# Turning tiles through DRAM instead of on TensorE in a four-layer graph kernel, with a fifth pair under way and an order by fitted keys

## Chip, cores, metric

One core of a Trainium2 chip. The metric is device time in us, the median of several executions. Every timed kernel ran on the same chip as runs of the kernel before. The runs are spread over several chips; the kernel before has medians of 3864.35 to 3866.42 us on them, so times from different chips compare to some 2 us. "Step" below always means the distance between successive elements of an operand within a partition, counted in fp32 elements of 4 bytes.

## The reference, cut

64 graphs of 256 nodes with 256 features pass four layers, each `x = x + layer(relu(layernorm(x)), adj)`, all in fp32:

```python
# layer 0: masked 8-head attention        q, k, v = h@Wq, h@Wk, h@Wv; softmax(where(adj>0, q k^T/sqrt(32), -1e9)) @ v @ Wo + bo
# layer 1: graph attention over columns   e = leaky(f1_i + f2_j); softmax over i; elu(att @ Wh)
# layer 2: gated graph network, 3 steps   m = A^T (h W_l);  h = GRU(m, h)
# layer 3: 4-head graph attention         probs = softmax(leaky(src_i + dst_j)); probs @ f
h = jnp.maximum(_layernorm(x, axis=-1), 0.0)
x = x + _L0_gnn_ref(h, adj, ...)     # and so on for layers 1, 2, 3
```

## The kernel before

Graphs are worked on in pairs, 512 tokens, as four chunks of 128 tokens; 32 pairs. Operations are added to a plan as tasks; a list scheduler in the host program fixes the order of all tasks on all engines, for four pairs under way at once (four token tiles `x`, thirty 128x1024 tiles `w4`). TensorE needs every normalised tile with features on the partitions, and layer 2's state with tokens on them. The kernel before gets both with TensorE's transposition:

```python
    def norm_relu_T(xt, p, tokens=False):
        ...                                       # statistics; xn = (x - mean) * rstd, tokens on partitions
        for k in range(2):
            ps = bank()
            def turn(k=k, ps=ps):                 # L554
                for t in range(T):
                    nc.tensor.transpose(ps()[:, t * P : (t + 1) * P], tok(xn())[:, t, k * P : (k + 1) * P], ident)
            add((PE, 4 * TURN, turn), reads=[xn], writes=[ps], claims=[hT])
            ...                                   # eviction with relu into hT[:, k, :], 512 tokens in a row
    def chunk(hT, k, t):                          # stationary operand: one chunk of 128 tokens
        return tok(hT(), N2)[:, k, t * P : (t + 1) * P]
    # layer 0, L662: mm(ps(), w[:, k, o*P:(o+1)*P], tok(hT(), N2)[:, k, :])        moving operand, 512 tokens
    # layer 2, L910: mm(ps(), w[:, k, c0:c0+P], at_o(src, k))                       moving operand, 512 tokens
    # layer 2, L891: mm(..., tok(h())[:, t, o*P:(o+1)*P], tok(am(), N)[:, t, :])    h as stationary operand
```

The attention probabilities of layers 0 and 3 were already turned in another way, by 32x32 blocks on VectorE and a round trip through DRAM that puts the blocks in their places:

```python
    def turn(e, eT, n):
        blocks = lambda: e().rearrange(f"p (r {n}) -> p r c i", c=2, i=32)
        add((V, dve(T * N), lambda: nc.vector.transpose(blocks(), blocks())), writes=[e])
        d = buf("turn")
        add((SP, 0.6, lambda: nc.sync.dma_start(d(), e())), reads=[e], writes=[d], latency=4.6)
        for b in range(4):
            add((SP, 0.55, lambda b=b: nc.sync.dma_start(
                    eT()[32 * b : 32 * b + 32, :].rearrange("p (a w) -> p a w", a=4),
                    d()[:, b * N : (b + 1) * N].rearrange("(a j) w -> j a w", a=4))),
                reads=[d], writes=[(eT, b)], latency=3.8)
```

## Time and profile before

| | before |
|---|---|
| time | 3866.03 us (3865.26 to 3868.96) |
| TensorE busy | 3785.4 us, 98% |
| VectorE, ScalarE busy | 77%, 57% |
| DMA queue's share of 16 engines; bytes | 45.9%; 554 MB |

In the views PE stands for TensorE's matmuls, PEld for its weight loads (they overlap matmuls), DVE for VectorE, ACT for ScalarE, POOL for GpSimd, SPq for SyncE's queue of transfers. L910 is line 910 of that run's kernel. A stretch view gives the stretch and its length, the busy us and count of PE, PEld, DVE, ACT and POOL, the granted clock, the DMA engines' share and GB/s.

Two rows of the groups by form (busy us, mean ns) are added for comparison with those after the change:

```profile
L910 PE MATMUL ps<-w,whhT 128*128 128x512 f32 x1536 | 725.2, 599 | 7.8 <-ACT w L336 7.5 <-DVE w L337 0.3
L788 PEld LDWEIGHTS ps<-w1a,w 128*128 128x128 f32 x512 | 97.2, 190 | 21.1 <-issue 7.2 <-ACT w L713 0.2 <-ACT w L563 0.2
```

TensorE's instructions in order of time (columns: start, length with the pipeline's drain, engine, line, operation, count). These are the query, key and value products:

```profile
2020.83 3.60 PE L662 MATMUL ps<-w,wq_sb 128*128 128x512 f32 x8
2024.26 3.60 PE L662 MATMUL ps<-w,wk_sb 128*128 128x512 f32 x8
2027.69 3.62 PE L581 MATMUL ps<-wv_sb,w 128*128 128x256 f32 x16
```

The cost of a group is the distance of its start from the next start: 3.43 us for eight, 0.429 us each. From such distances, each form's usual distance times its count, I get **3719 us of TensorE work** in the kernel before; the other 147 us of its 3866 are waits, most of them at the start and the end. (3719 is my reckoning from the trace; the rest of the text calls it "work", and time less work "waits".)

### The profile page before, as it was taken

The page shows a single profiled execution, that of the slowest core. Times are in us where ns is not written, and L with a number is a line of the kernel's source. Part 1 is how long each engine was busy: PE and PEld are TensorE (multiplying, and loading weights), DVE is VectorE, ACT ScalarE, POOL GpSimd, SP SyncE. Part 2 cuts the span into 40 slices and gives each one's busy share as a digit, 9 for nine tenths or more (in the row PEclk, how much of TensorE's full clock was granted, in tenths as well). Part 3 has the DMA queues.
Part 4 walks back from the last instruction along what each step waited for, and adds up shares of the span by engine and source line. Part 5 has one row for each costly group of instructions (what it writes and reads, how often), then busy time and mean ns, then how long its engine had stood idle before and what let it go on. Part 6 is the DMA issues. An engine that isn't in the chain of part 4 may idle for free.

```text
span 3862.9 us, 55709 instructions
## 1 busy us (share of the span) xinstructions
PE 3785.4 (98%) x17072; PEld 2286.4 (59%) x17072; DVE 2965.7 (77%) x8153; ACT 2211.7 (57%) x6139; POOL 673.9 (17%) x632
## 2 busy tenths in 40 slices
PE   8999999999999999999999999999999999999995
PEld 5665665565566566555666665656565665556553
DVE  7976778778877877787787788777787787877754
ACT  5745556555565555566555665555665556664632
POOL 1111211122111212111221112121111120111110
PEclk9999999999999999999999999999999999999997
DMA  7623444335453445453355444445544455444523
GB/s 226 186 92 102 153 148 152 125 120 178 158 156 113 150 137 164 151 167 124 116 163 159 156 131 149 138 145 169 154 126 132 133 176 164 149 135 122 157 66 99
DMA packets 402202, 554.29 MB, mean 143 GB/s; under 512 B 40304, under 2 KB 340208, under 8 KB 401904
## 3 DMA queue, kind: packets, MB, share of 16 engines
q1 hardware_dynamic: 401904, 550.73, 45.9%
q8 instruction: 137, 2.24, 0.2%
q14 instruction: 161, 1.32, 0.1%
HBM read 332.15 MB, written 218.43 MB: 143 GB/s over the span
## 4 chain that ended last, share of the span: by engine, by line
PE 95%; ACT 2%; DVE 1%; DMA 1%; SPq 0%; issue 0%; POOL 0%; POOLq 0%; ACTq 0%; DVEq 0%
PE ps L910 34%; PE ps L990 17%; PE ps L891 9%; PE ps L581 5%; PE ps L662 5%; PE ps L682 3%; PE ps L732 3%; PE ps L1119 3%; PE ps L1076 3%; PE ps L788 3%; PE ps L554 3%; PE ps L846 3%; PE ps L976 2%; ACT w L638 1%; PE ps L1134 1%; PE ps L431 0%
## 5 line engine op out<-in xcount | busy, mean ns | idle before, releaser
L638 ACT ACTIVATE w<-w,mx 128x256 f32<-128x256 f32 x1536 | 758.2, 500 | 22.8 <-DVE mx L630 22.8
L910 PE MATMUL ps<-w,whhT 128*128 128x512 f32 x1536 | 725.2, 599 | 7.8 <-ACT w L336 7.5
L910 PE MATMUL ps<-w,giT 128*128 128x512 f32 x1536 | 718.8, 595 | 0.0
L336 ACT COPY w<-ps 128x512 f32<-128x512 f32 x516 | 293.0, 583 | 442.4 <-PE ps L891 155.0
L614 DVE STREAM_TRANSPOSE w<-w 128x1024 f32<-128x1024 f32 x384 | 473.3, 1239 | 56.4 <-ACT w L638 46.7
L910 PEld LDWEIGHTS ps<-w,giT 128*128 128x128 f32 x1536 | 287.1, 190 | 337.8 <-issue 323.6
L910 PEld LDWEIGHTS ps<-w,whhT 128*128 128x128 f32 x1536 | 278.3, 191 | 292.5 <-issue 259.3
L630 DVE CUSTOM_DVE_ANT_0 w<-ps,mask 128x256 f32<-128x256 f32 x1024 | 370.1, 418 | 78.9 <-PE ps L682 78.5
L947 POOL TENSOR_TENSOR w<-w,w 128x512 f32<-128x512 f32 x128 | 165.3, 1297 | 1169.1 <-ACT w L942 944.8
L990 PE MATMUL ps<-whhT,w 128*128 128x512 f32 (+1 forms) x1024 | 360.8, 489 | 0.0
L990 PE MATMUL ps<-giT,w 128*128 128x512 f32 (+1 forms) x1024 | 360.0, 488 | 0.0
L891 PE MATMUL ps<-w,w 128*128 128x256 f32 x1536 | 348.4, 379 | 0.0
L891 PEld LDWEIGHTS ps<-w,w 128*128 128x128 f32 x1536 | 290.8, 190 | 56.6 <-issue 15.8
L638 ACT ACTIVATION_READ_ACCUMULATOR w<-w,mx 128x1 f32 x1536 | 296.5, 193 | 0.0
L990 PEld LDWEIGHTS ps<-giT,w 128*128 128x128 f32 x1024 | 192.3, 190 | 150.7 <-issue 129.0
L1023 ACT ACTIVATE w<-w 128x512 f32<-128x512 f32 x128 | 80.4, 628 | 306.4 <-DVE w L1019 306.2
L990 PEld LDWEIGHTS ps<-whhT,w 128*128 128x128 f32 x1024 | 189.2, 190 | 108.1 <-issue 89.7
L713 ACT ACTIVATE w<-w,rz 128x256 f32<-128x256 f32 x506 | 220.1, 501 | 26.8 <-DVE rz L706 26.5
L1044 POOL TENSOR_TENSOR w<-w,w 128x512 f32<-128x512 f32 x64 | 83.5, 1305 | 787.4 <-ACT w L1043 717.5
L1097 ACT ACTIVATE w<-w,f 128x256 f32<-128x256 f32 x512 | 217.3, 501 | 5.7 <-DMA w<-row 5.7
L922 ACT ACTIVATE w<-ps,brz 128x512 f32<-128x512 f32 x128 | 87.5, 684 | 230.4 <-PE ps L910 230.4
L1019 DVE TENSOR_TENSOR w<-ps,brz_bc 128x512 f32<-128x512 f32 x128 | 87.5, 684 | 155.2 <-PE ps L990 141.6
(122 smaller groups left out, 6084.3 us busy)
## 6 DMA issues: line engine op xcount, KB each, us to landing
turn<-w SPq DMA_DIRECT2D x384, 512.0 KB
w<-turn SPq DMA_DIRECT2D x1536, 128.0 KB
w<-in_adj_dram SPq DMA_DIRECT2D x128, 512.0 KB
w<-row SPq DMA_DIRECT2D x64, 512.0 KB
x<-in_x_dram SPq DMA_DIRECT2D x64, 256.0 KB
out_dram<-x SPq DMA_DIRECT2D x64, 256.0 KB
w<-row SPq DMA_DIRECT2D x32, 256.0 KB
w<-in_L_gnn_weight_dram SPq DMA_DIRECT2D x3, 256.0 KB
```

Of the source, the lines that this page charges most:

```text
L336: (A, act(n), lambda: nc.scalar.copy(dst(), src())),
L581: mm(ps()[:, c * D : (c + 1) * D], of(src, k, 2 * g + c), rhs[:, k, :], start=k == 0, stop=k == 1)
L614: add((V, dve(T * N), lambda: nc.vector.transpose(blocks(), blocks())), writes=[e])
L630: nc.vector.tensor_tensor_reduce(row, cols(src), cols(mask), scale, 3.0e38, ALU.add, ALU.min, mn)
L638: nc.scalar.activation(row, row, AF.Exp, bias=mn()[:, r : r + 1], scale=-1.0, accum_out=zs()[:, z0(r) : z0(r) + 1])
L662: mm(ps(), w[:, k, o * P : (o + 1) * P], tok(hT(), N2)[:, k, :], start=k == 0, stop=k == 1)
L713: op(row, row, rz()[:, r : r + 1])
L891: mm(ps()[:, g * N : (g + 1) * N], tok(h())[:, t, o * P : (o + 1) * P], tok(am(), N)[:, t, :], start=c == 0, stop=c == 1,)
L910: mm(ps(), w[:, k, c0 : c0 + P], at_o(src, k), start=n == 0, stop=n == 2 * len(terms) - 1)
L947: either(lambda eng, o=o, u=u, hT=hT, hn=hn: eng.tensor_sub(at_o(u, o), at_o(hT, o), at_o(hn, o))),
L990: mm(out, chunk(src, k, t), w[:, k, c0 : c0 + n], start=m == 0, stop=m == 2 * len(terms) - 1)
L1097: (A, act(N, 1), lambda t=t, g=g, h=h, e=e, r=r: nc.scalar.activation(rows_of(e())[:, r].rearrange("p b (c j) -> p c b j", c=2), sd[g]().r ...
```

## The change

It means to take the turnings off TensorE, the bound. In all pairs but the first and the last, normalised tiles of all layers and layer 2's states after steps 1 and 2 take the way of the probabilities. A fifth pair goes under way to cover the longer latency, and the order comes from fitted constants instead of 36 trials. Core of the diff, cuts marked:

```diff
-        "x": (4, [P, T * D], FP, 0),
-        "w4": (30, [P, T * D], FP, 9),
+        "x": (5, [P, T * D], FP, 0),
+        "w4": (29, [P, T * D], FP, 9),
...
+    def by_dma(what, p):
+        return 0 < p < B // 2 - 1
...                                        # norm_relu_T
+        if mixed:
+            turn_chunks(xn, hT)
+            return (at, hT, xn) if tokens else (at, hT)
...
+    def turn_chunks(src, dst):
+        e = w4()
+        turn_blocks(
+            dict(reads=[src], writes=[e]),
+            lambda: src().rearrange("p (x b j) -> p b x j", b=4, j=32),
+            lambda: e().rearrange("p (b i x) -> p b x i", b=4, i=32), dst,
+        )
+        dst.mixed = True
...
     def chunk(hT, k, t):
+        if hT.mixed:
+            return hT().rearrange("p (n x) -> p x n", x=2 * T)[:, 2 * t + k]
         return tok(hT(), N2)[:, k, t * P : (t + 1) * P]
+    def wide(hT, k):
+        if hT.mixed:
+            return hT().rearrange("p (n t k) -> p k t n", t=T, k=2)[:, k]
+        return tok(tok(hT(), N2)[:, k, :], P)
...                                        # layer 0 query, key; layer 2 gates
-                        mm(ps(), w[:, k, o * P : (o + 1) * P], tok(hT(), N2)[:, k, :], ...)
+                        mm(ps(), w[:, k, o * P : (o + 1) * P], wide(hT, k), ...)
...                                        # layer 2, after steps 1 and 2
+            if by_dma((2, l), p):
+                turn_chunks(u, h)
+                continue
...
-    order = plan.best([(s, d, f) for s in range(5, 11) for d in (2, 3) for f in (...)])
+        for do in plan.order():            # one order, keys from PERIOD, REST, ON_PE, ON_SP, OTHERS
```

The relu moves into the scaling, on ScalarE. And the turned tile interleaves eight chunks: token `n` of chunk and half `x` lies at element `8 n + x`. So successive tokens are at **step 8**, 32 bytes, wherever TensorE reads the tile. The layout has a reason: a stationary operand may have only one free dimension (a first attempt of mine with runs of 32 tokens as stationary operand was refused at the build with those words; that build is not among the recorded runs), and step 8 makes a chunk's 128 tokens one dimension.

The cut leaves out three smaller changes: layer 0's masks and probabilities take the layout in halves that layer 3's had, its value product loses the step of 2 of its stationary operand, and layer 2's last step holds one large tile more (`df`).

## The prediction

> **What bounds the kernel now.** I read the page's busy shares first, then its slices, then the chain that ended last, then the busy time by stretch, and last the order of TensorE's instructions in time.
>
> ```profile
> PE 3785.4 (98%) x17072; PEld 2286.4 (59%) x17072; DVE 2965.7 (77%) x8153; ACT 2211.7 (57%) x6139; POOL 673.9 (17%) x632
> ...
> PE   8999999999999999999999999999999999999995
> ...
> PE 95%; ACT 2%; DVE 1%; DMA 1%; SPq 0%; issue 0%; POOL 0%; POOLq 0%; ACTq 0%; DVEq 0%
> PE ps L910 34%; PE ps L990 17%; PE ps L891 9%; PE ps L581 5%; PE ps L662 5%; PE ps L682 3%; PE ps L732 3%; PE ps L1119 3%; PE ps L1076 3%; PE ps L788 3%; PE ps L554 3%; PE ps L846 3%; PE ps L976 2%; ACT w L638 1%; PE ps L1134 1%; PE ps L431 0%
> ```
>
> TensorE is busy 98% of the span, but busy time of matmuls has modelled ends, so the third and fourth lines are the stronger evidence: the chain goes back along TensorE for 95% of the span and hops to another engine almost only at its ends. On it stand L554 (turning of the normalised tiles, 3%) and L976 (turning of layer 2's state back to tokens, 2%). These two lines are what the change takes away. The busy time by stretch tells where TensorE is not full (the first numbers after the comma are PE busy):
>
> ```profile
> 0.00:100.00 100.00, 82.58 (x440) 53.55 (x441) 75.26 (x269) 60.75 (x190) 13.88 (x20) 0.93 0.74 224
> 1000.00:2000.00 1000.00, 996.36 (x4535) 602.74 (x4534) 787.67 (x2155) 573.39 (x1600) 184.78 (x170) 1.00 0.47 147
> 3780.00:3863.00 83.00, 42.74 (x159) 25.22 (x157) 34.57 (x80) 21.95 (x61) 6.24 (x6) 0.72 0.27 83
> ```
>
> In the middle TensorE stands still for 4 us in 1000; at the start and the end it is idle for some 20 and 40 us. The two pairs that the change leaves on TensorE are the first and the last, so those ends keep their shape. The order in time shows what one turning costs the engine:
>
> ```profile
> 2017.36 1.04 PE L554 MATMUL ps<-ident,w 128*128 128x128 f32 x8
> 2018.24 1.04 PE L976 MATMUL ps<-ident,w 128*128 128x128 f32 x8
> 2019.11 1.88 PE L910 MATMUL ps<-w,whhT 128*128 128x512 f32 x4
> ```
>
> The 1.04 us is length with the pipeline's drain. What the next group has to wait is the difference of the starts: 0.88 and 0.87 us for eight, so **0.109 us of TensorE per 128x128 turning**. In the same way L910's 512 columns cost 1.72 us for four, 0.43 us each.
>
> **What the Trainium skill says.** "Trainium Kernel Development and Optimization" (introduction, on reading a trace) calls matmul busy time a bad measure because matmuls are pipelined. The trace agrees: the rows give 599 ns for a 512-column matmul whose starts are 430 ns apart. So I count by starts.
> "SBUF — State Buffer" (Door 1, the note on cachelines) states 16-byte lines, that two hits on a line are needed for full bandwidth, and that a new line at each access pays. This is the main danger: the change lays a turned tile out so that successive tokens of a chunk lie 8 fp32, 32 bytes, apart, and TensorE reads it so, as moving and as stationary operand. The trace before has only steps of 2 elements: L732 reads its moving tile so, and pays nothing against L1119, which reads runs (391 and 394 ns in the rows). The stationary tile of wv is read at step 2 too; its weight load takes 196 ns against 190 at step 1. No run yet shows step 8. "TensorE: Matmul & The Clock Gate" (Weight-path and gap formulas) gives N/2.4 ns plus 2.5 for a warm matmul, 216 ns for 512 columns; here 430 ns. fp32 streams at half that rate, so one fp32 access takes about the time of two accesses at the page's rate. My estimate from this is that a new line per access just fits.
> "GPSIMD Engine Reference" (Performance pitfalls for Q7 kernels) says a step above 8 bytes costs some 50% more per element. The subtractions at L947 and L1044 take 1.3 us now; no trace yet shows the wide step.
>
> **The change, part by part.**
> 1. *TensorE loses.* From the instruction lists of both programs: L554's turnings go from 1024 to 64, L976's from 512 to 32. That is 1440 x 0.109 = **157 us** of TensorE. All other matmul counts are the same. Per pair it is 48 x 0.109 = 5.2 us; the pattern of long L910 groups in the chain repeats at 2744.30, 2978.18, 3212.06, thus each 233.9 us for two pairs, 117 us a pair, and should become about 111.7.
> 2. *TensorE's reads change.* If step 8 is free, nothing. See rival 1.
> 3. *VectorE.* 180 more 32x32-block turnings (384 to 564) at 473.3/384 = 1.23 us: +222. 360 fewer scalings (384 to 24) at 177.9/384 = 0.46: -167. About 55 fewer evictions with maximum at 0.68: -37; 33 fewer plain evictions at 0.68: -22. 74 more divisions by the row sum at 0.31: +23; 90 more bias columns at 0.16: +15; the layer-0 mask in two halves: +6. Sum +40 us: 3006 us, 81% of 3706. Still slack.
> 4. *ScalarE.* 360 more scalings with relu at 66.6/128 = 0.52: +187; about 127 fewer relu evictions at 0.56: -71; 148 fewer copies at 0.57: -84; 74 fewer divisions at 0.43: -32. Sum near 0: 60%.
> 5. *DMA.* 180 more round trips through DRAM, 0.5 MB each way: 189 MB on 554, to 743 MB. Over 3706 us this is 200 GB/s against 143; with 45.9% of the engines' time at 143 GB/s I estimate 64%. SyncE issues 3267 transfers for 2367; at a median of 0.43 us that is 1.4 ms, 38%.
> 6. *Latency.* The last round trip of the kernel before, with nothing beside it, shows what one costs: the block turning ends at 3842.1 us, its matmul starts at 3849.2, so 7 us, against some 2 us for turning and eviction on TensorE. Six per pair lengthen a pair by about 30 to 40 us. This is paid in buffers, not in time, as long as other pairs have work: four pairs at 117 us gave a pair 468 us; five at 112 give 558, 90 more.
> 7. *Order.* Instead of 36 orders tried there is one with keys fitted beforehand. The middle has 4 us in 1000 to win; the ends, some 20 and 40 us, may move by 10 us either way.
>
> Sum on the path that sets the end: 3863 - 157 = 3706 us. For waits on round trips with 29 instead of 30 large buffers and at a heavier DMA I add about 10 us, and some 2 for runs without profile: **3715 us**, 4% faster.
>
> **The rivals.**
> *Rival 1: the step of 32 bytes slows TensorE.* Moving reads concerned: L662's 512 and half of L910's whhT (768), in 30 of 32 pairs: 1200 x 0.43 = 515 us at today's rate. At half the rate the program would take 3706 + 515 = 4220 us. For it: the skill's page. Against it: the half rate of fp32 above, and that the authors kept the old lengths for these matmuls in their plan. Weight loads at step 8 (wv, L788, L1076, two thirds of L891, some 2400) lie beside matmuls of 216 ns and would have to double before they show. I give rival 1 in a harmful size 10%.
> *Rival 2: the DMA becomes the wait.* Landings grow late under 64% load, SyncE's queue is in order, and a transfer that waits for its block turning holds those behind it. For it: the kernel before already shows
>
> ```profile
> SPq L616 <- DVE w L614: 1014.9, 207, 38.2
> ...
> SPq L619 <- DMA turn<-w: 127.8, 76, 4.4
> ```
>
> a queue that stands a quarter of the span at the head of a round trip. Against it: TensorE's own waits do not feel it; the only large wait for DMA on TensorE is 23.7 us in all, in the tail. If it bites once per pair for 2 us, 3770 us; that is a gain of 2.5%.
> *Rival 3: VectorE or the buffers become the bound.* Its turnings write at step 8, and if each took double, VectorE would have 3228 us, 87%: late answers to TensorE, perhaps 3750 us. If the 29 buffers can't carry five pairs, the middle gets holes and the gain is half: 3785 us.
>
> **Range and chances.** The arithmetic of the removed work is sure to a few us; what is open is how much comes back. Rivals 2 and 3 at moderate size give 3740 to 3790; a better order at the ends gives 3680. Range 3670 to 3790. Faster by over 2% means below 3789: 0.84. Within 2%: 0.07. Slower: 0.09, nearly all of it rival 1.
>
> **What would show it.** Right: L554's and L976's successors shrink to 64 and 32 turnings; the starts of 512-column matmuls stay 0.43 us apart also on the turned tiles; the repeat per pair falls to about 112 us; TensorE stays at 97 to 98% and its chain near 95%; VectorE is at 80 to 82%, DMA at 60 to 66%. Step 2 is wrong if the first whhT product or the query product has longer matmuls than the others. Step 6 is wrong if TensorE waits in the middle for DMA of turned tiles. The prediction fails above 3790 us with TensorE well under 95%, or full with slower matmuls.

## The result, and the profile after

The changed kernel takes 4383.17 us (4380.96 to 4383.45) against 3866.03: ratio 1.1335, interval 1.1315 to 1.1354, **13% slower**, where 4% faster was predicted. Ratios here and below are the mean time of one kernel's fast runs over that of the other's of the same rounds, so not quite the ratio of the quoted medians.

From the page after (busy, and the chain that ended last):

```profile
PE 4271.6 (97%) x15632; PEld 2287.6 (52%) x15632; DVE 3114.7 (71%) x8101; ACT 2222.5 (51%) x6140; POOL 684.8 (16%) x625
...
PE 83%; DVE 7%; DMA 5%; SPq 2%; ACT 2%; issue 1%; POOL 0%; POOLq 0%; DVEq 0%; ACTq 0%
```

TensorE issues 1440 instructions less, as counted, and is 486 us longer busy. So it is still the bound, and its instructions have become longer. (The chain is on PE for 83% of the span and not for 95%. Steps to VectorE and DMA have come in, as they have in the fast program e_free below, 81%; so they do not carry the loss.) Its busy time in the middle says that it does not stand still:

```profile
1000.00:2000.00 1000.00, 994.44 (x3553) 523.85 (x3551) 717.22 (x1872) 513.97 (x1428) 161.36 (x144) 1.00 0.56 173
```

Which ones are longer, the groups by form tell (busy us, mean ns):

```profile
L933 PE MATMUL ps<-w,whhT 128*128 128x512 f32 x1536 | 1068.2, 834 | 2.5 <-issue 2.1 <-ACT w L315 0.2 <-DVE w L316 0.2
L933 PE MATMUL ps<-w,giT 128*128 128x512 f32 x1536 | 715.8, 595 | 0.0
L679 PE MATMUL ps<-w,wk_sb 128*128 128x512 f32 x256 | 233.8, 1065 | 0.0
L805 PEld LDWEIGHTS ps<-w1a,w 128*128 128x128 f32 x512 | 124.7, 325 | 17.5 <-issue 10.2 <-DVE w L961 3.4 <-ACT w L655 0.7
L606 DVE STREAM_TRANSPOSE w<-w 128x1024 f32<-128x1024 f32 x564 | 827.6, 1483 | 74.2 <-ACT w L521 59.4 <-ACT w L655 12.0 <-DMA w<-turn 1.0
```

L933 was L910 and reads two kinds of moving tile: with giT the messages, which TensorE made and which are contiguous (595 ns, as before); with whhT the state, in the first step a turned tile (834 ns in the mean of both steps; 599 before). L679 was L662 and reads nothing but turned tiles. In time:

```profile
2253.03 7.50 PE L679 MATMUL ps<-w,wq_sb 128*128 128x512 f32 x8
2260.35 7.52 PE L679 MATMUL ps<-w,wk_sb 128*128 128x512 f32 x8
2267.70 3.63 PE L863 MATMUL ps<-w,w 128*128 128x256 f32 x16
```

Eight take 7.32 to 7.35 us instead of 3.43: **0.918 us each instead of 0.429**. Of L933's 1536 with whhT, the trace has some 720 at that distance, half of the steps in 30 of 32 pairs. Weight loads from a turned tile take 325 ns instead of 190, and the matmuls of 256 to 264 columns that they feed come 0.239 us apart instead of 0.216 to 0.223. The sum over the trace:

| part | working | us |
|---|---|---|
| turnings taken off | 1440 x 0.109 | -157 |
| moving reads at step 8 | (480 of L679 + 720 of L933) x 0.489 | +587 |
| weight loads at step 8 | L572 480 x 0.024, L805 480 x 0.022, L1104 480 x 0.016, L914 960 x 0.023 | +52 |
| more waits | remainder: 4383 - 3866 + 157 - 587 - 52 | +35 |
| | | +517 |

So the table leaves TensorE with 3719 - 157 + 639 = 4201 us of work. (Expectations written during the study have 584 for 587, and 4342 for a sum that starts from the whole 3863 us, waits included.)

### The profile page after: what moved, and what is told of

It is laid out like the page before. It is cut to its first block, busy times and chain, and to the rows that moved or that the text cites. A ratio compares the mean times of both kernels' runs of the same rounds, so it can differ in the third digit from the quotient of the medians.

```text
span 4381.3 us, 54196 instructions
## 1 busy us (share of the span) xinstructions
PE 4271.6 (97%) x15632; PEld 2287.6 (52%) x15632; DVE 3114.7 (71%) x8101; ACT 2222.5 (51%) x6140; POOL 684.8 (16%) x625
## 4 chain that ended last, share of the span: by engine, by line
PE 83%; DVE 7%; DMA 5%; SPq 2%; ACT 2%; issue 1%; POOL 0%; POOLq 0%; DVEq 0%; ACTq 0%
PE ps L933 34%; PE ps L1022 10%; PE ps L679 10%; PE ps L914 6%; PE ps L572 5%; DMA w<-turn 4%; DVE w L606 3%; PE ps L699 3%; PE ps L805 3%; PE ps L1104 3%; PE ps L1147 2%; PE ps L863 2%; PE ps L749 2%; SPq L611 1%; DVE w L647 1%
## 5 line engine op out<-in xcount | busy, mean ns | idle before, releaser
L933 PE MATMUL ps<-w,whhT 128*128 128x512 f32 x1536 | 1068.2, 834 | 2.5 <-issue 2.1
L606 DVE STREAM_TRANSPOSE w<-w 128x1024 f32<-128x1024 f32 x564 | 827.6, 1483 | 74.2 <-ACT w L521 59.4
L933 PE MATMUL ps<-w,giT 128*128 128x512 f32 x1536 | 715.8, 595 | 0.0
L933 PEld LDWEIGHTS ps<-w,whhT 128*128 128x128 f32 x1536 | 293.4, 197 | 516.9 <-issue 487.6
L933 PEld LDWEIGHTS ps<-w,giT 128*128 128x128 f32 x1536 | 292.9, 193 | 464.0 <-issue 451.0
L315 ACT COPY w<-ps 128x512 f32<-128x512 f32 (+1 forms) x368 | 213.4, 582 | 609.9 <-PE ps L679 236.9
L970 POOL TENSOR_TENSOR w<-w,w 128x512 f32<-128x512 f32 x128 | 184.6, 1446 | 1390.3 <-ACT w L965 1302.2
L914 PE MATMUL ps<-w,w 128*128 128x256 f32 x1536 | 379.8, 397 | 1.2 <-DVE rz L723 1.2
L914 PEld LDWEIGHTS ps<-w,w 128*128 128x128 f32 x1536 | 345.9, 281 | 44.8 <-issue 17.7
L1022 PE MATMUL ps<-whhT,w 128*128 128x256 f32 (+1 forms) x1024 | 361.2, 490 | 0.0
L521 ACT ACTIVATE w<-x,rs 128x256 f32<-128x256 f32 x488 | 253.5, 589 | 168.8 <-DVE rs L512 147.0
L945 ACT ACTIVATE w<-ps,brz 128x512 f32<-128x512 f32 x128 | 87.8, 686 | 323.9 <-PE ps L933 312.9
L679 PE MATMUL ps<-w,wq_sb 128*128 128x512 f32 x256 | 233.4, 1064 | 4.6 <-DMA w<-turn 3.0
L977 ACT ACTIVATE w<-ps,brz 128x512 f32<-128x512 f32 x128 | 87.4, 685 | 295.6 <-PE ps L933 291.8
L679 PE MATMUL ps<-w,wk_sb 128*128 128x512 f32 x256 | 233.8, 1065 | 0.0
```

Of the source, the lines that this page charges most:

```text
L315: (A, act(n), lambda: nc.scalar.copy(dst(), src())),
L521: nc.scalar.activation(tok(xn())[:, t, :], tok(xt())[:, t, :], AF.Relu, bias=rs()[:, 1, t : t + 1], scale=rs()[:, 0, t : t + 1],)
L606: add((V, dve(T * N), lambda: nc.vector.transpose(dst(), src())), **e)
L679: mm(ps(), w[:, k, o * P : (o + 1) * P], wide(hT, k), start=k == 0, stop=k == 1)
L914: mm(ps()[:, g * N : (g + 1) * N], chunk_of(h, t, o), tok(am(), N)[:, t, :], start=c == 0, stop=c == 1,)
L933: mm(ps(), w[:, k, c0 : c0 + P], wide(src, k), start=n == 0, stop=n == 2 * len(terms) - 1)
```

## Experiments

Theory A: TensorE reads SBUF in 16-byte lines, and a moving operand pays when each element opens a new line. Theory B: it is the size of the step or a pattern of banks. Theory C (my rivals 2 and 3): the round trips, the fifth pair or the order cost the time, and the longer matmuls are a by-effect. All right results unless said.

### The step alone: e_sweep

The kernel before with wrong operands on purpose, each product on a line of its own, one execution (4144.3 us, state unknown; the readings compare lines of this one trace):

```diff
-                        mm(ps(), w[:, k, o * P : (o + 1) * P], tok(hT(), N2)[:, k, :], ...)
+                        mm(ps(), wk, spaced(hT, 2, k, 1), ...)      # then 4, 8, 16 for the next products
...                                                                  # layer 2, first step, whhT:
+ mm(ps(), wk, src().rearrange("p (n s e) -> p s n e", s=4, e=2)[:, 2*k : 2*k+2], ...)   # L947 runs of 2, every 8
+ mm(ps(), wk, src().rearrange("p (n s e) -> p s n e", s=2, e=4)[:, k], ...)             # L949 runs of 4, every 8
+ mm(ps(), wk, src().rearrange("p (n s e) -> p s n e", s=2, e=2)[:, k], ...)             # L951 runs of 2, every 4
+ mm(ps(), wk, src()[:, 0:768].rearrange("p (n s) -> p s n", s=3)[:, k : k+2], ...)      # L953 step 3; L955 step 6
+ mm(ps(), wk, src().rearrange("p (a t k i) -> p k t a i", a=4, t=T, k=2)[:, k], ...)    # L957 runs of 32
...                                                                  # value product, stationary operand at steps 1 to 8
+ mm(o, columns_of(src, 4), rhs[:, k, :], ...)
```

> The kernel before, with wrong operands on purpose (same tiles, same sizes): the four query and key products read their moving operand at steps of 2, 4, 8 and 16 fp32; the first whhT products of layer 2 read runs of 2 at step 8, runs of 4 at step 8, runs of 2 at step 4, step 3, step 6 and runs of 32 (step 256); the wv products read their stationary operand at steps 1 to 8. Theory A (a new 16-byte line per element is what costs): moving reads are 0.43 us from start to start at step 2, at runs of 2, 4 and 32, and about 0.92 at steps 4, 6, 8 and 16, with step 3 between (three elements of four open a new line); weight loads near 195 ns up to step 2 and near 330 from step 4 on. Theory B (the size of the step or a bank pattern costs): the time grows with the step, step 4 lies well below 8, step 16 above it, and odd or non-power-of-two steps (3, 5, 6, 7) are cheap.

The groups by form (L690, L692, L694, L696 are steps 2, 4, 8, 16):

```profile
L694 PE MATMUL ps<-w,wk_sb 128*128 128x512 f32 x128 | 123.3, 1098 | 0.0
L692 PE MATMUL ps<-w,wq_sb 128*128 128x512 f32 x128 | 120.3, 1073 | 0.0
L696 PE MATMUL ps<-w,wk_sb 128*128 128x512 f32 x128 | 115.4, 1034 | 0.0
L953 PE MATMUL ps<-w,whhT 128*128 128x512 f32 x128 | 91.8, 844 | 0.0
L690 PE MATMUL ps<-w,wq_sb 128*128 128x512 f32 x128 | 65.2, 631 | 2.8 <-ACT w L563 2.7
L947 PE MATMUL ps<-w,whhT 128*128 128x512 f32 x128 | 65.0, 629 | 0.0
L957 PE MATMUL ps<-w,whhT 128*128 128x512 f32 x128 | 63.9, 622 | 0.0
L951 PE MATMUL ps<-w,whhT 128*128 128x512 f32 x128 | 63.1, 614 | 0.0
L949 PE MATMUL ps<-w,whhT 128*128 128x512 f32 x128 | 60.2, 592 | 0.0
```

The rows' means carry drain. From start to start, median:

| moving operand | new 16-byte lines per element | us per 512 columns |
|---|---|---|
| step 1; runs of 4 every 8; runs of 32 | 1/4 | 0.429 |
| step 2; runs of 2 every 4; runs of 2 every 8 | 1/2 | 0.451; 0.450; 0.458 |
| step 3 | 3/4 | 0.675 |
| step 4; 6; 8; 16 | 1 | 0.900; 0.897; 0.918; 0.858 |

The count of new lines orders all eleven; the size of the step does not (runs of 2 every 8 cost half of step 4, and step 16 is a little cheaper than step 8). Between 1/2 and 1 the time runs in a straight line: step 3 lies midway, at 0.675. **Theory A stands, B falls**: step 6 is as dear as 4. The weight loads (duration min/median/max; steps 2, 3, 4, 8 in this order):

```profile
L594 PEld LDWEIGHTS ps<-wv_sb,w x64: 193/195/197, 24.5 to 3816.6; 128*128 128x128 f32 x64
L596 PEld LDWEIGHTS ps<-wv_sb,w x64: 251/251/253, 25.0 to 3817.0; 128*128 128x128 f32 x64
L598 PEld LDWEIGHTS ps<-wv_sb,w x64: 307/317/329, 25.4 to 3817.4; 128*128 128x128 f32 x64
L606 PEld LDWEIGHTS ps<-wv_sb,w x64: 334/335/338, 27.2 to 3819.3; 128*128 128x128 f32 x64
```

The same law; but a load lies beside the matmul of 256 columns, and what comes through is small: 0.216 us from start to start up to step 3, 0.223 to 0.233 at steps 4 to 7, 0.240 at step 8.

### One factor in the changed kernel: e_runs2

```diff
-            lambda: e().rearrange("p (b i x) -> p b x i", b=4, i=32), dst,
+            lambda: e().rearrange("p (b x i) -> p b x i" if runs else "p (b i x) -> p b x i", b=4, i=32), dst,
...                                     # runs: layer 2's normalised tile alone
+        if hT.mixed == "runs":
+            return hT().rearrange("p (a t k i) -> p k t a i", a=4, t=T, k=2)[:, k]
```

This tile is read only as moving operand (and by one subtraction), and a moving operand may have several free dimensions. Turnings, round trips and order stay.

> The changed kernel with one thing altered: layer 2's normalised tile comes back in runs of 32 (the block turning writes it so). Same turnings, same round trips, same order of all instructions. If the step of the moving operand is the cause, 720 matmuls fall from 0.918 to 0.429 us: 352 us off, 4031 us, and the block turnings of these tiles fall from 2.0 to 1.2 us on VectorE. If the round trips are the cause, it stays at 4383.

4035.04 us, 348 us below the changed kernel, 352 expected. The rows of it for the matmuls in question and the block turnings:

```profile
L939 PE MATMUL ps<-w,whhT 128*128 128x512 f32 x1536 | 716.3, 598 | 2.8 <-issue 2.0 <-DVE w L316 0.4 <-ACT w L315 0.2
L608 DVE STREAM_TRANSPOSE w<-w 128x1024 f32<-128x1024 f32 x564 | 804.0, 1441 | 72.2 <-ACT w L521 54.5 <-ACT w L657 11.8 <-DMA w<-turn 3.5
```

834 ns are back at 598. This is the cause shown in place: two thirds of the whole loss hang on how one tile is laid out. (The 30 block turnings of this tile get shorter too, 24 us of VectorE's busy time in all, so they cannot be the 348.) Theory C is out as the main cause.

### What the change would have given with free reads: e_free and e_free_tried

Wrong results: the changed kernel with the same round trips, buffers and order, but every read of a turned tile contiguous. The block turnings write runs too, and take 1.23 us instead of 2.0; so e_free frees VectorE of some 143 us as well, and does not separate the two effects.

```diff
-            lambda: e().rearrange("p (b i x) -> p b x i", b=4, i=32), dst,
+            lambda: e().rearrange("p (b x i) -> p b x i", b=4, i=32), dst,
-        dst.mixed = True
```

> The changed kernel with the same turnings, round trips, buffers and order, but every read of a turned tile contiguous (wrong results on purpose: tokens and features are mixed up; the block turnings write runs of 32). If the wide step is the whole of my error, this is 3715 us as predicted. From e_no_dma and e_runs2, which keep 190 to 250 us of waits under this order, I now expect 3719 - 157 + 190 = 3750 us.

3740.51 us, ratio 0.967 (0.9654 to 0.9687). Its page and its middle:

```profile
PE 3633.3 (97%) x15632; PEld 2134.1 (57%) x15632; DVE 2972.0 (79%) x8101; ACT 2204.1 (59%) x6140; POOL 650.9 (17%) x625
```

```profile
1000.00:2000.00 1000.00, 993.15 (x4264) 581.87 (x4263) 819.58 (x2215) 609.16 (x1694) 185.87 (x178) 1.00 0.68 209
```

So the rest of the sum held: work 3719 - 157 = 3562, waits 179 instead of 147.

> e_free with its order found by the 36 trials. If the order by keys makes the extra waits, this falls to 3562 + 125 = 3690 us (125 us of waits is what e_five and e_after_tried keep); if the round trips make them, it stays near e_free.

3752.72 us: **missed** by some 60. For the program that it was made for, the order by keys is as good as 36 trials. Neither order gets rid of the extra waits; that the round trips make them fits this, but a better order, which no run looked for here, is not excluded.

### Order and fifth pair, without round trips: e_no_dma, e_five

e_no_dma is the changed kernel with `by_dma` returning `False`; e_five is the kernel before with the changed numbers of tiles, its order found by the 36 trials.

> The changed kernel with its order, its five pairs and its layouts of masks and probabilities, but every turning on TensorE as before. If the wide step of the turned tiles is the cause of the loss, this is near the kernel before: 3850 to 3890 us. If the order by keys or the fifth pair costs, it is 3950 us or more.

> The kernel before with nothing changed but five token tiles and 29 large ones (five pairs under way), its order found by the 36 trials as before. e_no_dma lost 110 us with no turning moved: if the fifth pair does that, this is near 3975 us too; if the order by keys does it, this stays within 20 us of the kernel before, at 3850 to 3880.

e_no_dma: 3974.88 us, ratio 1.0283, so 110 us worse than before, and 135 worse than e_five, with the same TensorE work. e_five: 3839.77 us, ratio 0.9934, 25 us less than before, with five pairs and the order that the trials found for them. (25 us is no more than orders of one program differ by, below.) The middle of both, e_no_dma first:

```profile
1000.00:2000.00 1000.00, 965.56 (x4297) 580.01 (x4295) 746.84 (x2054) 526.35 (x1444) 169.79 (x157) 0.99 0.45 137
```

```profile
1000.00:2000.00 1000.00, 1000.00 (x4544) 606.08 (x4543) 770.69 (x2149) 610.59 (x1695) 175.18 (x170) 1.00 0.46 146
```

e_five's busy time shows no hole in the middle; e_no_dma leaves 34 us in 1000. The likely reason is that the keys do not carry over to a program with other latencies. It is not shown alone: e_no_dma also has the changed kernel's layouts of masks and its tile `df`, and no run has these with the 36 trials and without round trips. e_l2_tried below has them, with the trials and one such tile a pair through DRAM, and takes 3840 us, so most of the 135 us is the order's. For the changed kernel itself the order's part is smaller:

> The changed kernel, layouts as changed, with its order found by the 36 trials, the slow matmuls given at their measured length. The arithmetic of the parts (3863 - 157 + 584 + 52 = 4342) leaves some 40 us of the changed kernel to waits. If these are the keys' order, made for matmuls of half the length, this is near 4320; if they come with the round trips, it stays within 15 us of 4383.

4322.76 us. An order found by trials, with the true lengths of the slow matmuls, takes 60 us off, to 4201 + 122. The keys had been made with 0.43 us for matmuls that take 0.92; whether the trials or the lengths did it is not separated.

### The stationary reads and a repaired version: e_state, e_mix, and their orders

```diff
# e_state: only layer 2's states through DRAM (stationary at step 8)
-        return 0 < p < B // 2 - 1
+        return isinstance(what, tuple) and 0 < p < B // 2 - 1
# e_mix: layer 0 on TensorE; layer 2's tile in runs (as in e_runs2); layers 1, 3 and the states at step 8
+        return what != 0 and 0 < p < B // 2 - 1
# e_l2_tried: what == 2;  e_l2st_tried: what == 2 or isinstance(what, tuple)
# *_tried: the kernel before's Plan with its 36 trials;  e_mix_tried4: four pairs, 30 tiles
```

> The changed kernel with only layer 2's tokens turned through DRAM: no moving operand at the wide step is left, only stationary ones. 480 turnings less are 52 us off, 960 matmuls at 239 instead of 216 ns are 22 us on: 30 us below e_no_dma. If the loss lay in the DMA round trips or in the stationary reads, a third of the loss (170 us) would be here.

> The changed kernel with layer 0 turned on TensorE and layer 2's normalised tile laid out in runs of 32 (it is read only as moving operand); layers 1 and 3 and the states stay at the wide step as stationary operands. If the step of the moving operand is the cause, all of the 587 us goes and the time is about 3780 us (3863 less 5 x 8 x 30 turnings at 0.109 us = 131, plus some 45 for the weight loads). If the round trips themselves are the cause, it stays above 4100 us.

e_state 3921.60, 53 us below e_no_dma (30 expected: the difference of work is 30, the rest is fewer waits); e_mix 3846.20, ratio 0.995. No moving read at a wide step is left in either, and the 13% are gone; but e_mix missed its 3780. Its waits are some 218 us, so the next runs vary what could make them wait.

> e_mix with its order found by the 36 trials of the kernel before in place of the keys; all else the same, five pairs. TensorE has 86 us less to do than before (131 us of turnings off, 45 us of slower stationary reads on); if the keys' order is what keeps e_mix at 3846, this is 3770 to 3790. If the round trips cause the waits, it stays near 3840.

> The same with four pairs under way and 30 large tiles. If the fifth pair is needed to cover the longer latency of the round trips, 20 us or more slower than e_mix_tried; else equal.

> e_five with only layer 2's normalised tile turned through DRAM, in runs of 32, so that no operand of TensorE stands at a wide step: 240 turnings off at no price on TensorE, 26 us below e_five: 3814 us. If e_mix_tried's 25 us above its arithmetic come from the number of round trips or VectorE's share, this one with a fifth of them gets its full 26 us.

> The same with layer 2's states through DRAM too (stationary, at the wide step): 480 more turnings off are 52 us, 960 weight loads too long for their matmul are 22 us on: 30 us below e_l2_tried, 3784 us, if TensorE stays full; above 3800 if the round trips make it wait.

e_mix_tried 3816.33 (0.9876), missed its 3770 to 3790. e_mix_tried4 3964.75 (1.0257): with the round trips, **four pairs are 148 us worse than five**. e_l2_tried 3840.17 (0.993): missed, the 26 us less of work do not show against e_five. (The expectation calls it e_five with one tile turned otherwise; it also carries the changed kernel's mask layouts and `df`.) e_l2st_tried 3817.86 (0.9875): missed its 3784. Last, e_all_tried is e_mix_tried with layer 0's tile also in runs and the value product made of four 32-column stationary tiles, each one run:

> e_mix_tried with layer 0's tile also turned through DRAM, in runs of 32: query and key products read it as moving operand, and the value product loads it as four 32-column stationary tiles beside each other. 240 turnings less are 26 us off; the column tiles cost 0.03 us for each of 480 matmuls, 13 us: about 13 us below e_mix_tried. If VectorE or the queue is the limit by then, it is equal or slower.

3824.18 (0.9894): a miss too, some 8 us slower instead of 13 faster. The column tiles are not to blame: in the trace a set of four starts every 0.216 us, as one matmul of 256 columns does with a contiguous stationary tile, and 0.024 less than at step 8. With orders picked from some 3600, and with measured lengths for the slower reads and block turnings:

```diff
-    order = plan.best([(s, d, f) for s in range(5, 11) for d in (2, 3) for f in (...)])
+    order = plan.best([(5, 2, (2, 0, 3, 2))])         # e_l2st_sought, with OTHERS = (2, 1, 0, 1)
```

> e_mix_tried (right results) with an order picked from some 3600 instead of 36 and with measured lengths of the slower stationary reads and block turnings. If its 180 us of waits are the order's, it falls to 3633 + 125 = 3760 us; if they are the round trips' or VectorE's, it stays within 15 us of 3816.

> e_l2st_tried with an order picked in the same way. TensorE's work is 3719 - 26 - 52 + 22 = 3663 us; with 125 us of waits 3788, against 3818 now; within 15 us of 3818 if the waits are not the order's.

e_mix_sought 3799.61 (0.983, 0.9815 to 0.9844) lies between its two forecasts, nearer to the one for waits that are not the order's. e_l2st_sought is **3796.16 us (0.9821, 0.981 to 0.984)**, 8 us above the forecast for waits that are: the best of all with right results, 13% faster than the changed kernel and 1.8% faster than the one before. The gain over the one before is clear of noise but under 2%. The middle, e_mix_tried first, then e_l2st_tried and e_l2st_sought:

```profile
1000.00:2000.00 1000.00, 987.47 (x4214) 605.86 (x4211) 809.48 (x2148) 605.80 (x1690) 181.77 (x169) 1.00 0.62 192
```

```profile
1000.00:2000.00 1000.00, 991.19 (x4327) 597.62 (x4326) 818.21 (x2182) 580.83 (x1635) 173.63 (x163) 1.00 0.57 173
1000.00:2000.00 1000.00, 1000.00 (x4362) 603.18 (x4361) 811.91 (x2213) 607.09 (x1690) 175.72 (x167) 1.00 0.57 176
```

VectorE is as busy in all three (81 to 82%); so it is not its share alone that makes TensorE wait. In e_l2st the other order, with truer lengths, closed the holes. In e_mix it did not: e_mix_sought has 988.06 us of busy TensorE in the same stretch, though it is 17 us faster in all.

The runs by TensorE's work and waits (work of e_runs2 and of the runs with round trips is reckoned from the parts above, not counted anew):

| run | TensorE work, us | time, us | waits, us |
|---|---|---|---|
| before | 3719 | 3866 | 147 |
| e_five | 3719 | 3840 | 121 |
| e_no_dma | 3719 | 3975 | 256 |
| e_state | 3689 | 3922 | 233 |
| e_l2_tried | 3693 | 3840 | 147 |
| e_l2st_tried / e_l2st_sought | 3663 | 3818 / 3796 | 155 / 133 |
| e_mix / e_mix_tried / e_mix_sought | 3628 | 3846 / 3816 / 3800 | 218 / 188 / 172 |
| e_mix_tried4 | 3628 | 3965 | 337 |
| e_all_tried | 3602 | 3824 | 222 |
| e_free / e_free_tried (wrong results) | 3562 | 3741 / 3753 | 179 / 191 |
| e_runs2 | 3849 | 4035 | 186 |
| after / e_after_tried | 4201 | 4383 / 4323 | 182 / 122 |

Among orders found by the 36 trials for five pairs, the more tiles take the round trip and the shorter TensorE's work, the more waits, but for e_free_tried; the two change together, so which of them it is stays open. With TensorE the slowest by far (e_after_tried) there are none beyond those of e_five.

"Waits" is a remainder, and not all of it is idle time. The traces have short stretches in which the granted clock is 0.5, and there 512-column matmuls start 0.853 us apart instead of 0.429. The mean granted clock is 0.992 in e_five and 0.984 in e_no_dma, 0.988 in e_mix_tried and 0.975 in e_mix_tried4. By my estimate from these shares and the spans that is at most 33 of the 135 us and 53 of the 148 us between them.

## Why the prediction was wrong, point by point

**The step that failed is part 2, "TensorE's reads change. If step 8 is free, nothing."** I had named its failure as rival 1, with its source in the skill's page, and then given it 10%. The argument that made it small was: "fp32 streams at half that rate, so one fp32 access takes about the time of two accesses at the page's rate ... a new line per access just fits." (The page has that rate under "Back-to-back issue gap"; the prediction gives the section another name.) It does not fit: at that half rate a new line per element takes 0.858 to 0.918 us per 512 columns instead of 0.429, and the step of 2 that the trace before showed to be free has only half a new line per element. The sign that I named for this, TensorE "full with slower matmuls", is what came. That the plan's own lengths for these matmuls were unchanged was no evidence either; they were wrong by a factor of two. Rival 1's size, 515 us, was near: 587 measured, since the factor is 2.14 and not 2. What I did not count is the weight loads, 52 us: I wrote that they "would have to double before they show"; 325 ns for 190 already showed, with 0.016 to 0.024 us a matmul. (In e_sweep 251 ns still hid behind the matmul of 256 columns, and 317 did not.)

**Part 1 was right**: 64 and 32 turnings left, and e_free gives the effect of the 157 us.

**Part 3, VectorE**: 3006 us predicted, 3115 measured, mostly because a block turning that writes at step 8 takes 2.0 us, not 1.23 (rival 3 had doubled it, 3228). Where it writes runs, in e_free, VectorE is at 2972.

**Parts 4 and 5**: 2212 us of ScalarE predicted, 2222 measured; 743 MB and 64% of the DMA engines predicted for 3706 us, 743 MB and 64.2% in e_free. Rival 2 did not come as put: TensorE's waits for round-trip tiles, other than the one long wait of the tail, stay small, some 17 us in the changed kernel and 15 in e_free. Still e_free waits 179 us in all, 32 more than the kernel before and 58 more than e_five, where the prediction's sum added 10 for what **part 6** describes, and named "four pairs gave a pair 468 us ... five give 558" as the cover. The cover is needed (e_mix_tried4, one order for each number of pairs); that the round trips are what costs the rest is argued, not shown. The chain, forecast "near 95%", is at 83%, and at 81% in e_free.

**Part 7, order**: "may move by 10 us either way". It moves 60 us in the changed kernel itself, 12 in e_free, and most of 135 between e_five and e_no_dma.

Without the failed step the prediction would have stood: e_free's 3740.5 us lies in its range and 26 us above its 3715. Some of that nearness may be luck: e_free's block turnings are freed too, and the fifth pair, a gain that the prediction counted only as cover, came with 25 us less in e_five.

Left open: why e_l2_tried gets nothing of its 26 us (the order, the mask layouts and `df` are all possible; the run that would tell, the changed kernel without round trips under the 36 trials, was not made), and how much of the 58 us of waits in e_free beyond e_five's a better order could close. Two orders of one program lie 12 us (e_free), 22 (e_l2st), 17 and 30 (e_mix) and 60 us (changed kernel) apart here, so single runs of this kind don't settle differences of some 25 us.

## What to carry to other kernels

When a layout is changed to make a transfer or a turning cheap, price the reads at the new step before anything else: the fp32 moving operands here ran at nearly full speed with two elements in each 16-byte line, and at half speed with one. A moving operand took runs in several free dimensions here. A stationary one had to be a single step at the build, and four column tiles of 32, each a run, did the same work in 0.216 us (e_all_tried). A run with wrong operands and one source line per step gives the price in a single trace. Where one engine is full, count its work by distances of starts and watch "time less work": it separates what an operation costs from what an order or a latency costs.

## What the Trainium skill lacked or had wrong

- "SBUF — State Buffer", Door 1, the cachelines: that two hits on a line are needed for full bandwidth is nearly right for fp32 moving operands (0.451 us at two hits, 5% over the 0.429 at four; 0.900 at one). Its addition that one can stride for free up to 4 fp32 is wrong here: step 3 costs 0.675 and step 4 0.900. The size of the penalty, 2.1 times for matmuls, is on no page.
- "TensorE: Matmul & The Clock Gate", LDWEIGHTS: the time is given from the columns alone, 107 ns for 128. In fp32 a load of 128 columns took 190 ns here with a contiguous stationary tile, and 251, 317 and 335 ns at step 3, 4 and 8.
- No page that I read states that the stationary operand must have exactly one free dimension; the build refused an operand with two.
- "VectorE: DVE Perf Modes", The three transpose paths: no word on the destination's step. A 128x1024 block turning took 1.24 us into runs or step 2 and 2.0 us into step 8.
- "GPSIMD Engine Reference", Performance pitfalls for Q7 kernels: 50% more for a step above 8 bytes. A subtraction of 128x512 with one operand of two at step 8 took a median of 1532 ns (L1077 of the changed kernel) against 1277 without (the same line in e_no_dma), 20% more.
